# A GAT layer and a relational attention layer in one kernel: the second feed-forward's second product computed from seven products of quarters

## The chip, the cores and the metric

The kernel runs on one core of one Trainium2 chip. Five engines work side by side, each through its own list of instructions: TensorE (PE in the profile, its weight loads PEld), VectorE (DVE), ScalarE (ACT), GpSimd (POOL) and SyncE (SP), which here issues transfers. The metric is the time of one execution on the device in microseconds (us).

## The reference

64 graphs of 256 nodes with 256 features pass through two layers. In what follows, `x` is [64, 256, 256] and `adj` a 0/1 matrix per graph, all in float32:

```python
# layer 0
h = gat(x, adj, W1, a1);  h = gat(h, adj, W2, a2)     # softmax of leaky_relu scores
h = layernorm(x + h)
h = layernorm(h + relu(h @ w_ff1 + b_ff1) @ w_ff2 + b_ff2)
# layer 1, 8 heads of 32, relations r = 0..3
attn = softmax(q k^T / sqrt(32))
out  = sum over r of (attn * (adj == r)) @ v_r
x  = layernorm(h + out @ Wo + bo)
ff = gelu(x @ W1 + b1) @ W2 + b2        # 256 -> 1024 -> 256: W2 is what the change is about
return layernorm(x + ff)
```

## The kernel before, in words

Two graphs make a unit: 512 rows, in T = 4 blocks of 128 tokens, and there are NG = 32 units. `turn(y_, x_, z)` (L1021 to L1128) runs 32 times and works on three units at once: y does the attention and the second feed-forward (layer 1), x = y+1 the first feed-forward, z = y+2 the two GAT steps. `y`, `X["y"]` and so on are also the names of the residual rows of such a unit, [128, 4, 256], to which each stage adds in place. A prologue ahead of the turns (the fill) does units 0 and 1 and folds the scales and shifts of the layer norms into the weights, in pieces (`folding`, advanced by `next(fold)`).

A turn starts with `queries_keys` (qp, kp), then the scores of one graph and four heads at a time (sp, exponentials e, masked ea, sums es), the values (vp, v), the sums over the heads (po, zo), and, between these, x's first product (h1p). Then come z's projection (xpp), y's output product (yop), x's second product (yfp with wf), y's first product of the second feed-forward, then z's second GAT step, and y's second product (yfp with w).

The first product of the second feed-forward (`hidden_seven`, L789 to L870) already takes Strassen's seven products of quarters: the weights' combinations are made once in the fill (`seven`), those of the moving features by VectorE in each turn, and the results are added by VectorE and ScalarE from two PSUM banks per half. The second product (`hidden_out_block`, L872 to L882) is the plain one: for each block of 128 tokens eight matmuls over the 1024 hidden features, each with 128 tokens as the stationary operand and 256 columns of w2 moving; a float32 matmul shows as two records in the trace. At the end of each pair of blocks VectorE adds the bank to y (L882).

In the last part of a turn, the order is as follows. `hidden_seven` ends with z's `gat_first` between its parts. x's rows are normed (`normed`, L752 to L771: statistics and their aggregate by VectorE, rs by GpSimd, nm by VectorE, four scalings y by ScalarE), and brought into feature order by `normed_features` (four VectorE transposes into yt, then 16 moves of 32-row blocks, as SP transfers where `natural` is set). x's `affine` (rg2, rb2; two VectorE operations of 128x1024) follows, then z's `second_scores` (rows by TensorE, softmax by ScalarE and VectorE, which ends by scaling hp). `finish` norms and writes out the unit y-1, which was put in `waiting` a turn before. Then the product of y goes through its four blocks, and ahead of the last block `second_sums(z)` runs: ygp, two adds to z's rows, z's first norm, and `normed_features`, in which 4 of the 16 moves are GpSimd copies hT<-yt and 12 are SP transfers. These transposed rows of z are wanted in the middle of the next turn. z's next affine (rg1, rb1) comes after y's second norm there.

The order on PE and SP is the order of the program's text. On VectorE, ScalarE and GpSimd a scheduler chooses it from the times that it expects; `with behind(mark)` holds an instruction back until the marked one has been issued. PSUM has six banks that are shared in turn (tag "g"), and two more (po, zo). A matmul that takes a bank waits until the reader of what was in it has finished. Tiles of a tag with two buffers (`work`) are reused in turn in the same way.

The last two units differ: unit 30's product is cut into `pieces`, which are drawn one at a time within the last turn, and unit 31 has none beside it.

Of the kernel before, what the change touches and what calls it, by code (L numbers as in the profile page):

```python
# [9 lines left out]
F32 = mybir.dt.float32  # L10
# [375 lines left out]
def narrow_path(  # L386
# [97 lines left out]
    def columns(vs, name, queue):  # L484

        ns = [v.shape[0] // P for v in vs]
        rows = work.tile([P, KB * N], F32, tag="rz", name=f"{name}r")[:, 0:P]
        t = const.tile([P, sum(ns)], F32, name=name)
        at, views = 0, []
        for v, n in zip(vs, ns):  # L490
            queue.dma_start(rows[at:at + n, :], v.rearrange("(c p) -> c p", p=P))
            views.append(t[:, at:at + n])
            at += n
        ps = bank(f"{name}p")
        nc.tensor.transpose(ps[:, :at], rows[:at, :], ident[:at, :at])
        nc.vector.tensor_copy(t, ps[:, :at])
        return views
# [61 lines left out]
    def seven(w, name):  # L559
# [8 lines left out]
        nc.gpsimd.tensor_tensor(a21, a11, a21, ALU.subtract)  # L568
        return a11, a12, a22, s1, s2, a21, s4


    def shifted(w, blocks, shift, bias, name):
        ps = bank(f"{name}sp{blocks[0]}")
# [8 lines left out]
        for k in range(KB):  # L582
            nc.gpsimd.tensor_scalar(w[:, k], w[:, k], scale[:, k:k + 1], 1.0, op0=ALU.mult, op1=ALU.mult)

    w1s = []

    def folding():

        shifted(wf1, range(FB // 2), lb1, bf1, "bf1")
        yield  # L590
        shifted(wf1, range(FB // 2, FB), lb1, bf1, "bf1")
        scaled(wf1, lg1)
        yield
# [12 lines left out]
        shifted(w1, range(FB // 2, FB), lb3, b1, "b1")  # L606
        scaled(w1, lg3)
        w1s.extend(seven(w1, "w1"))
        yield

    fold = folding()


    for rb, v, name in ((rb1, g_bf2, "rbf2"), (rb2, t_bo, "rbo"), (rb3, t_b2, "rbt2")):
        nc.gpsimd.tensor_add(rb, rb, row(v, name, work.tile([P, KB * N], F32, tag="rz", name=name)[:, :F]))


    mark = {}
# [8 lines left out]
    def to_features(src, name):  # L627

        dst = work.tile([P, KB, TN], F32, tag="hT", name=name)
        for k in range(KB):  # L630
            ps = bank(f"{name}p{k}")
            for t in range(T):
                nc.tensor.transpose(ps[:, t * P:(t + 1) * P], src[:, t, k * P:(k + 1) * P], ident)
            nc.vector.tensor_copy(dst[:, k, :], ps)
        return [dst[:, k] for k in range(KB)]

    def adjacency(u, aq):
# [5 lines left out]
    def normed_features(u, l, xn, natural=False, queues=(nc.sync,)):  # L643
# [7 lines left out]
        if natural:  # L651
            hT = work.tile([P, KB, TN], F32, tag="hT", name=f"hT{u}_{l}")
            to = hT.rearrange("c k (t a r) -> c (k t) a r", a=Q, r=32)
            for q in range(Q):
                for a in range(Q):
                    nc.sync.dma_start(to[q * 32:(q + 1) * 32, :, a],
                                      yt[a * 32:(a + 1) * 32, q].rearrange("c k t r -> c (k t) r"))
            return [hT[:, k] for k in range(KB)]
        hT = work.tile([P, Q, KB, T, 32], F32, tag="hT", name=f"hT{u}_{l}")
        n = 0  # L660
# [80 lines left out]
    def add_blocks(u, name, y, b, lhs, rhs, n):  # L741

        ps = bank(f"{name}{u}_{b}")
        for i in range(NB):
            t = b * NB + i
            for k in range(n):
                nc.tensor.matmul(ps[:, i * F:(i + 1) * F], lhs(t, k), rhs(b, k),  # L747
                                 start=(k == 0), stop=(k == n - 1))
        yb = y[:, b * NB:(b + 1) * NB, :].rearrange("p t f -> p (t f)")
        nc.vector.tensor_tensor(yb, ps, yb, ALU.add)  # L750

    def normed(u, l, y, blocks=range(T)):  # L752

# [36 lines left out]
    def hidden_seven(u, l, hT, w, bi, func, h1):  # L790
# [58 lines left out]
        for h in halves:  # L849
            product(two[h], h, s1, moving(0), True)  # L850
            p5[h] = copied(h, 1, two[h])
        for h in halves:
            product(two[h], h, s4, quarter[1][1], False)
            copied(h, 0, two[h])
# [8 lines left out]
        for h in halves:  # L863
            product(one[h], h, s3, moving(2), False)
            added(h, 1, 1, p5[h])
        yield
        for h in halves:
            product(one[h], h, a22, moving(3), False)
            done(h, 1, 0, one[h])
            done(h, 1, 1)  # L870

    def hidden_out_block(u, l, y, h1, wo_, t):  # L872
        b, i = divmod(t, NB)
# [6 lines left out]
        if i == NB - 1:  # L880
            yb = y[:, b * NB:(b + 1) * NB, :].rearrange("p t f -> p (t f)")
            nc.vector.tensor_tensor(yb, ps, yb, ALU.add)  # L882

    hidden_ps = {}

# [65 lines left out]
                             start=True, stop=True)  # L951

    def divided(u, b, po, zo, oT):
        rz = work.tile([P, KB * N], F32, tag="rz", name=f"rz{u}_{b}")
        nc.vector.reciprocal(rz, zo)  # L955
        nc.vector.tensor_tensor(oT[:, :, b * N:(b + 1) * N],
                                po.rearrange("p (m n) -> p m n", m=KB),
# [25 lines left out]
    def first_scores(z):  # L983
        first_rows(z)
        first_softmax(z)

    def second_scores(z):
        d = g[z]
        d["s"] = gat_softmax(z, 1, d["hp"], score_rows(z, 1, d["hp"], F), F + 1, F, d["aT"])

    def second_sums(x_, on_tensor=False):
        d = g[x_]
# [9 lines left out]

    left = []

    def out_pieces(u, y, h1):

        for t in range(T):
            hidden_out_block(u, 1, y, h1, w2, t)
            b, i = divmod(t, NB)
            if i == NB - 1:  # L1010
                finish(u, y, b, 1)
            yield

    def finish(u, y, b, n):

        bt = slice(b * NB, (b + n) * NB)
        normed(u, 3, y, range(b * NB, (b + n) * NB))
        with behind("added"):
            affine(y[:, bt, :], rg4, rb4)
        nc.sync.dma_start(out[G * u + b:G * u + b + n].rearrange("b (c p) f -> p (b c) f", p=P), y[:, bt, :])  # L1020

    def piece():
# [3 lines left out]
    def turn(y_, x_, z):  # L1026
# [19 lines left out]
        def first_hidden(blocks):  # L1046
            if X:
                X["h1"] = hidden(x_, 0, X["hT"], wf1, bf1, AF.Relu, blocks, X.get("h1"))

        scores(0)  # L1050
        v = values(y_, hT, range(T))
# [46 lines left out]
            if Z and n > 1:  # L1098
                Z["hp"] = gat_first(z, Z["s"], Z["xp"], Z.get("hp"), range(2 * n - 4, 2 * n - 2))
        if X:  # L1100
            with behind("copied"):
                normed(x_, 1, X["y"])
            X["hT"] = (normed_features(x_, 1, X["y"], natural=True) if Z
                       else to_features(X["y"], f"h2T{x_}"))
            with behind("added"):
                affine(X["y"], rg2, rb2)
        if Z:
            checked(z, Z["aq"])
        if z + 1 < NG:
            load_adjacency(z + 1)  # L1110
        if Z:
            second_scores(z)
        if waiting:
            with behind("scaled" if Z else "copied"):
                finish(*waiting.pop(), 0, G)
        if y_ >= NG - 2:
            last = out_pieces(y_, y, h1)
            if X:
                left.append(last)
            else:  # L1120
                for _ in last:
                    pass
            return
        for t in range(T):
            if t == T - 1:
                second_sums(z)
            hidden_out_block(y_, 1, y, h1, w2, t)
        waiting.append((y_, y))  # L1128

    waiting = []  # L1130
# [4 lines left out]
    with tc.manual_schedule(engines={mybir.EngineType.PE, mybir.EngineType.SP}):  # L1135
# [18 lines left out]
        h1 = hidden(0, 0, g[0]["hT"], wf1, bf1, AF.Relu, range(FB))  # L1154
        hidden_out(0, 0, g[0]["y"], h1, wf2)
        normed(0, 1, g[0]["y"])
        next(fold)
        second_sums(1)
        g[0]["hT"] = to_features(g[0]["y"], "h2T0")
        affine(g[0]["y"], rg2, rb2)  # L1160
        for u in range(NG):
            turn(u, u + 1, u + 2)

# [53 lines left out]
```

## Time and profile before

| | us |
|---|---|
| median of 3 runs | 3192.44 (3191.73 to 3194.73) |
| profiled execution, time | 3190.37 |
| profiled execution, span | 3188.7 |
| mean granted TensorE clock in it | 0.993 of full speed |
| one turn (382.26 to 478.84, from the start of y's second product to that of the next) | 96.6 |
| VectorE busy | 2117.7 (66% of the span) |
| ScalarE busy | 1547.8 (49%) |
| GpSimd busy | 412.1 (13%) |

In the profile's rows, "yfp<-w,h" is y's second product, "yfp<-wf,h" that of x, L878 the line of both; "x2048" counts records, and "128*128 128x256" gives the tile of the stationary operand and the shape of the result. "idle before <-releaser" is what the engine waited for just ahead of the instruction. A row of the timeline has start, length, engine, line, operation, names and count; matmuls are pipelined, so the length of a row of them runs over the start of the next row a little, and the time that a row takes is best read from start to start. The waits of the whole kernel that belong to the places of the change:

```profile
POOL rs L763 <- DVE mv L762: 1743.8, 97, 52.1
ACT y L768 <- DVE nm L765: 420.2, 69, 20.8
POOL hT L665 <- DVE yt L648: 166.1, 56, 3.6
DVE nm L765 <- POOL rs L764: 160.6, 129, 2.1
ACT k L899 <- PE kp L897: 47.2, 62, 1.0
PEld h1a L820 <- DVE h L830: 16.6, 33, 1.2
PE qp L897 <- DVE h2T L634: 6.3, 2, 6.0
```

Its columns are: who waits, for whom, the sum in us, how many times, the longest. None of the first five is a wait of TensorE.

### The profile page before, as it was taken

To read this page: it belongs to the slowest core of one execution; us is meant where nothing else is said; L and a number is where in the kernel's file an instruction comes from. 1 tells how busy PE (TensorE), PEld (TensorE's weight loads), DVE (VectorE), ACT (ScalarE), POOL (GpSimd) and SP (SyncE) were. 2 spreads that over 40 slices of the span, in tenths; PEclk is the share of its full clock that TensorE was granted. 3 is DMA by queue.
4 is the path that set the end of the run, shared out by engine and by line. 5 is a ranking of instruction groups with operands and counts; after the bars stand their busy time and mean duration, and the time that the engine had idled before them with its cause. 6 is when DMAs were issued, how large, how long until landed. Compare 5 with 4: busy or idle time off the path is not lost.

```text
span 3188.7 us, 46935 instructions
## 1 busy us (share of the span) xinstructions
PE 3137.3 (98%) x17584; PEld 2178.4 (68%) x17584; DVE 2117.7 (66%) x3870; ACT 1547.8 (49%) x3076; POOL 412.1 (13%) x633
## 2 busy tenths in 40 slices
PE   8899999999999999999999999999999999999997
PEld 5577766677766677666677666777666776667755
DVE  3566666666676666676666666666766666766655
ACT  4255544555544545545545445554445455455543
POOL 1111011011011111110110110110101111101100
PEclk9999999999999999999999999999999999999999
DMA  5011112121111121121211121211112111211000
GB/s 144 19 37 37 21 35 44 39 44 29 26 39 40 42 44 26 24 43 39 44 37 22 34 44 39 44 29 24 40 39 44 40 28 25 44 39 31 24 12 15
DMA packets 461160, 117.09 MB, mean 37 GB/s; under 512 B 397400, under 2 KB 460288, under 8 KB 460928
## 3 DMA queue, kind: packets, MB, share of 16 engines
q1 hardware_dynamic: 450592, 106.60, 15.4%
q10 hardware_dynamic: 9280, 6.39, 0.7%
q8 instruction: 141, 2.31, 0.3%
q0 software_dynamic: 1056, 1.05, 0.1%
q14 instruction: 91, 0.75, 0.1%
HBM read 57.04 MB, written 16.78 MB: 23 GB/s over the span
## 4 chain that ended last, share of the span: by engine, by line
PE 91%; DVE 4%; ACT 1%; POOL 1%; DMA 1%; ACTq 1%; issue 1%; SPq 0%; DVEq 0%; POOLq 0%
PE yfp L878 24%; PE h1p L785 14%; PE po L947 7%; PE vp L910 7%; PE h1a L820 6%; PE sp L926 4%; PE h1b L820 4%; PE qp L897 4%; PE yop L747 4%; PE kp L897 3%; PE hpp L736 3%; PE xpp L694 3%; PE ygp L747 3%; PE zo L950 2%; POOL rs L764 1%; DVE st L761 1%
## 5 line engine op out<-in xcount | busy, mean ns | idle before, releaser
L934 DVE TENSOR_TENSOR ea<-e,aT 128x1024 f32<-128x1024 f32 x256 | 302.2, 1222 | 285.1 <-ACT e L932 285.1
L768 ACT ACTIVATE y<-y,nm,rs 128x256 f32<-128x256 f32 x512 | 269.4, 591 | 420.2 <-DVE nm L765 420.2
L878 PE MATMUL yfp<-w,h 128*128 128x256 f32 x2048 | 452.9, 379 | 0.0
L785 PE MATMUL h1p<-hT,wf 128*128 128x512 f32 x992 | 450.6, 602 | 0.0
L878 PE MATMUL yfp<-wf,h 128*128 128x256 f32 x2048 | 448.5, 380 | 0.0
L878 PEld LDWEIGHTS yfp<-wf,h 128*128 128x128 f32 x2048 | 387.8, 191 | 52.2 <-issue 0.5
L878 PEld LDWEIGHTS yfp<-w,h 128*128 128x128 f32 x2048 | 386.6, 190 | 51.9 <-DVE v L912 0.3
L932 ACT ACTIVATE e<-sp 128x512 f32<-128x512 f32 x512 | 263.7, 603 | 224.4 <-PE sp L926 218.1
L785 PEld LDWEIGHTS h1p<-hT,wf 128*128 128x128 f32 x992 | 180.6, 189 | 228.7 <-issue 193.1
L648 DVE STREAM_TRANSPOSE yt<-y 128x256 f32<-128x256 f32 x368 | 151.7, 431 | 214.7 <-ACT y L768 201.0
L787 ACT ACTIVATE h<-h1p,cols 128x512 f32<-128x512 f32 x256 | 172.8, 692 | 239.0 <-PE h1p L785 239.0
L763 POOL TENSOR_SCALAR rs<-mv 128x4 f32<-128x4 f32 (+1 forms) x130 | 29.1, 232 | 1751.0 <-DVE mv L762 1743.8
L955 DVE RECIPROCAL rz<-zo 128x512 f32<-128x512 f32 x64 | 214.7, 3354 | 53.6 <-PE zo L950 53.6
L665 POOL COPY hT<-yt 32x256 f32<-32x256 f32 x248 | 215.8, 870 | 191.9 <-DVE yt L648 166.1
L775 DVE TENSOR_TENSOR y<-y,rg 128x1024 f32<-128x1024 f32 (+1 forms) x130 | 157.0, 1209 | 98.5 <-ACT y L768 94.2
L910 PE MATMUL vp<-wv,hT 128*128 128x512 f32 x480 | 214.0, 599 | 0.0
L761 DVE BATCH_NORM_STATS2 st<-y 128x6 f32<-128x256 f32 x512 | 195.3, 408 | 4.5
L826 ACT COPY cp<-h1b 128x512 f32<-128x512 f32 x192 | 111.1, 581 | 113.4 <-PE h1b L820 70.1
L910 PEld LDWEIGHTS vp<-wv,hT 128*128 128x128 f32 x480 | 88.7, 190 | 110.4 <-issue 103.2
L776 DVE TENSOR_TENSOR y<-y,rb 128x1024 f32<-128x1024 f32 (+1 forms) x130 | 161.2, 1242 | 3.2
L830 DVE TENSOR_TENSOR h<-h1a,cp 128x512 f32<-128x512 f32 x192 | 130.3, 682 | 45.7 <-PE h1a L820 45.6
L696 ACT COPY xp<-xpp 128x260 f32<-128x260 f32 x128 | 47.6, 373 | 232.6 <-PE xpp L694 232.5
(183 smaller groups left out, 4773.1 us busy)
## 6 DMA issues: line engine op xcount, KB each, us to landing
hT<-yt SPq DMA_DIRECT2D x1038, 32.0 KB, 1.9
y<-in_x_dram SPq DMA_DIRECT2D x32, 512.0 KB, 4.0
xq<-in_x_dram SPq DMA_DIRECT2D x240, 64.0 KB, 2.3
aq<-in_adj_dram SPq DMA_DIRECT2D x240, 64.0 KB, 2.4
out_dram<-y SPq DMA_DIRECT2D x30, 512.0 KB
hT<-yt ACTq DMA_DIRECT2D x186, 32.0 KB, 1.9
wf<-in_L_gnn_w_ff_dram SPq DMA_DIRECT2D x2, 1024.0 KB, 7.1
w<-in_L_gnn_W_dram SPq DMA_DIRECT2D x2, 1024.0 KB
```

The costliest lines, as they stand in the source:

```text
L665: nc.gpsimd.tensor_copy(to, at)
L747: nc.tensor.matmul(ps[:, i * F:(i + 1) * F], lhs(t, k), rhs(b, k), start=(k == 0), stop=(k == n - 1))
L761: nc.vector.bn_stats(st[:, t, :], y[:, t, :])
L768: mark["normed"] = nc.scalar.activation(y[:, t, :], y[:, t, :], AF.Identity, bias=nm[:, t:t + 1], scale=rs[:, t:t + 1])
L785: nc.tensor.matmul(ps, wi[:, k, f * P:(f + 1) * P], hT[k], start=(k == 0), stop=(k == KB - 1))
L820: nc.tensor.matmul(ps[:, i * N:(i + 1) * N], w_[:, f * P:(f + 1) * P], m, start=first and i == 0, stop=True, skip_group_check=True)
L878: nc.tensor.matmul(ps[:, i * F:(i + 1) * F], h1[:, k, t * P:(t + 1) * P], wo_[:, k, :], start=(k == 0), stop=(k == FB - 1))
L897: nc.tensor.matmul(ps, w[:, k, m * P:(m + 1) * P], hT[k], start=(k == 0), stop=(k == KB - 1))
L910: nc.tensor.matmul(ps, hT[k][:, t * P:(t + 1) * P], wvf[:, k, :], start=(k == 0), stop=(k == KB - 1))
L932: nc.scalar.activation(e[:, a, :], ps[a], AF.Exp, scale=isd)
L934: nc.vector.tensor_tensor(ea[:, a:a + 2, :], e[:, a:a + 2, :], ab[:, None, :].to_broadcast([P, 2, NB * N]), ALU.mult)
L947: nc.tensor.matmul(po[hp, m * N:(m + 1) * N], vs[:, hp], w[:, a, j * N:(j + 1) * N], start=(n == 0), stop=(n == len(terms) - 1))
```

## The change

The second product of the second feed-forward is computed from seven products of quarters, too (`hidden_out_seven`). The hidden features h1 are cut into four quarters (first or second half of the 1024 features, first or second graph of the unit); VectorE makes four combinations s1, s2, s4, s3 of them in each turn, of 128x1024 elements, and the weights' combinations t1, t2, t3, t4 are made once by GpSimd in the fill (`seven_out`). A product is eight matmuls with 128 tokens stationary and 128 columns of weights moving, into one bank. Products 1, 4, 6 and 7 share one bank, 3 and 5 another, product 2 has its own; a product that adds to a bank starts after VectorE has added what was there before to the residual rows.

Around it:
- z's ygp sums come after the sixth product, where they came ahead of the last quarter of the plain one, and z's `second_softmax` is issued after the third.
- x's norm is behind the mark "fifth" in place of "copied"; of the 16 moves of its features the four with equal source and target rows become GpSimd copies.
- x's affine (rg2, rb2), and after it the `finish` of unit y-1, are issued after the products, behind the marks "summed" (the last add of ygp) and "quarters" (s3).
- done(h, 1, 1) in `hidden_seven` stands one part earlier.
- `to_features`, which takes transposes by TensorE out of PSUM in the fill and at the end, copies by ScalarE in place of VectorE; in the fill, `next(fold)` of the last part comes behind it; in turn 31 the pieces of unit 30 are drawn in more places.
- the tag "rz" has one buffer in place of two.

```diff
@@ -568,6 +568,18 @@
         nc.gpsimd.tensor_tensor(a21, a11, a21, ALU.subtract)
         return a11, a12, a22, s1, s2, a21, s4
 
+    def seven_out(w, name):
+
+        h = F // 2
+        b11, b12, b21, b22 = (w[:, k * FB // 2:(k + 1) * FB // 2, o * h:(o + 1) * h]
+                              for k in range(2) for o in range(2))
+        t1, t2, t4 = (const.tile([P, FB // 2, h], F32, name=f"{name}t{n}") for n in (1, 2, 4))
+        nc.gpsimd.tensor_tensor(t1, b12, b11, ALU.subtract)
+        nc.gpsimd.tensor_tensor(t2, b22, t1, ALU.subtract)
+        nc.gpsimd.tensor_tensor(t4, b21, t2, ALU.subtract)
+        nc.gpsimd.tensor_tensor(b12, b22, b12, ALU.subtract)
+        return b11, b21, b22, t1, t2, b12, t4
+
 
     def shifted(w, blocks, shift, bias, name):
         ps = bank(f"{name}sp{blocks[0]}")
@@ -582,7 +594,7 @@
         for k in range(KB):
             nc.gpsimd.tensor_scalar(w[:, k], w[:, k], scale[:, k:k + 1], 1.0, op0=ALU.mult, op1=ALU.mult)
 
-    w1s = []
+    w1s, w2s = [], []
 
     def folding():
 
@@ -606,13 +618,14 @@
         shifted(w1, range(FB // 2, FB), lb3, b1, "b1")
         scaled(w1, lg3)
         w1s.extend(seven(w1, "w1"))
+        w2s.extend(seven_out(w2, "w2"))
         yield
 
     fold = folding()
 
 
     for rb, v, name in ((rb1, g_bf2, "rbf2"), (rb2, t_bo, "rbo"), (rb3, t_b2, "rbt2")):
-        nc.gpsimd.tensor_add(rb, rb, row(v, name, work.tile([P, KB * N], F32, tag="rz", name=name)[:, :F]))
+        nc.gpsimd.tensor_add(rb, rb, row(v, name, work.tile([P, KB * N], F32, tag="rz", name=name, bufs=1)[:, :F]))
 
 
     mark = {}
@@ -631,7 +644,7 @@
             ps = bank(f"{name}p{k}")
             for t in range(T):
                 nc.tensor.transpose(ps[:, t * P:(t + 1) * P], src[:, t, k * P:(k + 1) * P], ident)
-            nc.vector.tensor_copy(dst[:, k, :], ps)
+            nc.scalar.copy(dst[:, k, :], ps)
         return [dst[:, k] for k in range(KB)]
 
     def adjacency(u, aq):
@@ -653,8 +666,8 @@
             to = hT.rearrange("c k (t a r) -> c (k t) a r", a=Q, r=32)
             for q in range(Q):
                 for a in range(Q):
-                    nc.sync.dma_start(to[q * 32:(q + 1) * 32, :, a],
-                                      yt[a * 32:(a + 1) * 32, q].rearrange("c k t r -> c (k t) r"))
+                    move = nc.gpsimd.tensor_copy if q == a else nc.sync.dma_start
+                    move(to[q * 32:(q + 1) * 32, :, a], yt[a * 32:(a + 1) * 32, q].rearrange("c k t r -> c (k t) r"))
             return [hT[:, k] for k in range(KB)]
         hT = work.tile([P, Q, KB, T, 32], F32, tag="hT", name=f"hT{u}_{l}")
         n = 0
@@ -747,7 +760,7 @@
                 nc.tensor.matmul(ps[:, i * F:(i + 1) * F], lhs(t, k), rhs(b, k),
                                  start=(k == 0), stop=(k == n - 1))
         yb = y[:, b * NB:(b + 1) * NB, :].rearrange("p t f -> p (t f)")
-        nc.vector.tensor_tensor(yb, ps, yb, ALU.add)
+        mark["summed"] = nc.vector.tensor_tensor(yb, ps, yb, ALU.add)
 
     def normed(u, l, y, blocks=range(T)):
 
@@ -849,6 +862,7 @@
         for h in halves:
             product(two[h], h, s1, moving(0), True)
             p5[h] = copied(h, 1, two[h])
+        mark["fifth"] = mark["copied"]
         for h in halves:
             product(two[h], h, s4, quarter[1][1], False)
             copied(h, 0, two[h])
@@ -863,11 +877,11 @@
         for h in halves:
             product(one[h], h, s3, moving(2), False)
             added(h, 1, 1, p5[h])
+            done(h, 1, 1)
         yield
         for h in halves:
             product(one[h], h, a22, moving(3), False)
             done(h, 1, 0, one[h])
-            done(h, 1, 1)
 
     def hidden_out_block(u, l, y, h1, wo_, t):
         b, i = divmod(t, NB)
@@ -880,6 +894,54 @@
         if i == NB - 1:
             yb = y[:, b * NB:(b + 1) * NB, :].rearrange("p t f -> p (t f)")
             nc.vector.tensor_tensor(yb, ps, yb, ALU.add)
+
+    def hidden_out_seven(u, l, y, h1, w, s1, s2, s3, s4):
+
+
+        b11, b21, b22, t1, t2, t3, t4 = w
+        K2, F2 = FB // 2, F // 2
+        a11, a12, a21, a22 = (h1[:, k * K2:(k + 1) * K2, b * N:(b + 1) * N]
+                              for b in range(2) for k in range(2))
+        nc.vector.tensor_tensor(s1, a21, a22, ALU.add)
+        nc.vector.tensor_tensor(s2, s1, a11, ALU.subtract)
+        nc.vector.tensor_tensor(s4, a12, s2, ALU.subtract)
+        mark["quarters"] = nc.vector.tensor_tensor(s3, a11, a21, ALU.subtract)
+
+        def product(ps, a, w_, first):
+            for i in range(NB):
+                for k in range(K2):
+                    nc.tensor.matmul(ps[:, i * F2:(i + 1) * F2], a[:, k, i * P:(i + 1) * P], w_[:, k, :],
+                                     start=first and i == 0 and k == 0, stop=True, skip_group_check=True)
+
+        def added(b, o, ps):
+            yq = y[:, b * NB:(b + 1) * NB, o * F2:(o + 1) * F2]
+            nc.vector.tensor_tensor(yq, ps[:, :F].rearrange("p (i f) -> p i f", i=NB), yq, ALU.add)
+
+        n = f"{l}_{u}"
+        one = bank(f"yf1{n}")
+        product(one, a11, b11, True)
+        added(0, 0, one)
+        yield
+        two = bank(f"yf3{n}")
+        product(two, s1, t1, True)
+        added(1, 1, two)
+        yield
+        ps = bank(f"yf2{n}")
+        product(ps, a12, b21, True)
+        added(0, 0, ps)
+        yield
+        product(one, s2, t2, False)
+        added(0, 1, one)
+        yield
+        product(two, s4, b22, False)
+        added(0, 1, two)
+        yield
+        product(one, s3, t3, False)
+        added(1, 1, one)
+        yield
+        product(one, a22, t4, False)
+        added(1, 0, one)
+        yield
 
     hidden_ps = {}
 
@@ -984,9 +1046,16 @@
         first_rows(z)
         first_softmax(z)
 
+    def second_rows(z):
+        g[z]["rows"] = score_rows(z, 1, g[z]["hp"], F)
+
+    def second_softmax(z):
+        d = g[z]
+        d["s"] = gat_softmax(z, 1, d["hp"], d["rows"], F + 1, F, d["aT"])
+
     def second_scores(z):
-        d = g[z]
-        d["s"] = gat_softmax(z, 1, d["hp"], score_rows(z, 1, d["hp"], F), F + 1, F, d["aT"])
+        second_rows(z)
+        second_softmax(z)
 
     def second_sums(x_, on_tensor=False):
         d = g[x_]
@@ -1002,21 +1071,25 @@
 
     left = []
 
-    def out_pieces(u, y, h1):
-
-        for t in range(T):
-            hidden_out_block(u, 1, y, h1, w2, t)
-            b, i = divmod(t, NB)
-            if i == NB - 1:
-                finish(u, y, b, 1)
+    def out_pieces(u, y, h1, last):
+
+
+        if u == NG - 2:
+            s = [work.tile([P, T, N], F32, tag="s", name=f"sq{u}_{n}") for n in range(2)]
+            s += [io.tile([P, T, N], F32, tag=t, name=f"sq{u}_{t}", bufs=1) for t in ("xq", "aq")]
+        else:
+            s = [work.tile([P, HPB, NB * N], F32, tag=t, name=f"{t}q{u}")[:, :, i * N:(i + 1) * N]
+                 for t in ("e", "ea") for i in range(2)]
+        for n, _ in enumerate(hidden_out_seven(u, 1, y, h1, w2s, *s)):
+            if last and n in (4, 6):
+                finish(u, y, n // 6, 1)
             yield
 
     def finish(u, y, b, n):
 
         bt = slice(b * NB, (b + n) * NB)
         normed(u, 3, y, range(b * NB, (b + n) * NB))
-        with behind("added"):
-            affine(y[:, bt, :], rg4, rb4)
+        affine(y[:, bt, :], rg4, rb4)
         nc.sync.dma_start(out[G * u + b:G * u + b + n].rearrange("b (c p) f -> p (b c) f", p=P), y[:, bt, :])
 
     def piece():
@@ -1046,6 +1119,8 @@
         def first_hidden(blocks):
             if X:
                 X["h1"] = hidden(x_, 0, X["hT"], wf1, bf1, AF.Relu, blocks, X.get("h1"))
+            else:
+                piece()
 
         scores(0)
         v = values(y_, hT, range(T))
@@ -1098,33 +1173,34 @@
             if Z and n > 1:
                 Z["hp"] = gat_first(z, Z["s"], Z["xp"], Z.get("hp"), range(2 * n - 4, 2 * n - 2))
         if X:
-            with behind("copied"):
+            with behind("fifth"):
                 normed(x_, 1, X["y"])
             X["hT"] = (normed_features(x_, 1, X["y"], natural=True) if Z
                        else to_features(X["y"], f"h2T{x_}"))
-            with behind("added"):
-                affine(X["y"], rg2, rb2)
         if Z:
             checked(z, Z["aq"])
         if z + 1 < NG:
             load_adjacency(z + 1)
         if Z:
-            second_scores(z)
-        if waiting:
-            with behind("scaled" if Z else "copied"):
-                finish(*waiting.pop(), 0, G)
-        if y_ >= NG - 2:
-            last = out_pieces(y_, y, h1)
-            if X:
-                left.append(last)
-            else:
-                for _ in last:
-                    pass
+            second_rows(z)
+        pieces = out_pieces(y_, y, h1, y_ >= NG - 2)
+        if y_ == NG - 2:
+            left.append(pieces)
+            affine(X["y"], rg2, rb2)
+            finish(*waiting.pop(), 0, G)
             return
-        for t in range(T):
-            if t == T - 1:
+        for n, _ in enumerate(pieces):
+            if Z and n == 2:
+                second_softmax(z)
+            if Z and n == 5:
                 second_sums(z)
-            hidden_out_block(y_, 1, y, h1, w2, t)
+        if not X:
+            return
+        with behind("summed", "quarters"):
+            affine(X["y"], rg2, rb2)
+            if waiting:
+                with behind("scaled"):
+                    finish(*waiting.pop(), 0, G)
         waiting.append((y_, y))
 
     waiting = []
@@ -1154,10 +1230,10 @@
         h1 = hidden(0, 0, g[0]["hT"], wf1, bf1, AF.Relu, range(FB))
         hidden_out(0, 0, g[0]["y"], h1, wf2)
         normed(0, 1, g[0]["y"])
-        next(fold)
         second_sums(1)
         g[0]["hT"] = to_features(g[0]["y"], "h2T0")
         affine(g[0]["y"], rg2, rb2)
+        next(fold)
         for u in range(NG):
             turn(u, u + 1, u + 2)
```

More of the change, by code (lines that the diff above doesn't have):

```diff
@@ L486, in columns @@
         ns = [v.shape[0] // P for v in vs]
-        rows = work.tile([P, KB * N], F32, tag="rz", name=f"{name}r")[:, 0:P]
+        rows = work.tile([P, KB * N], F32, tag="rz", name=f"{name}r", bufs=1)[:, 0:P]
         t = const.tile([P, sum(ns)], F32, name=name)
@@ L953, in divided @@
     def divided(u, b, po, zo, oT):
-        rz = work.tile([P, KB * N], F32, tag="rz", name=f"rz{u}_{b}")
+        rz = work.tile([P, KB * N], F32, tag="rz", name=f"rz{u}_{b}", bufs=1)
         nc.vector.reciprocal(rz, zo)
```

## The prediction, before the result was known

> **What bounds the kernel.** I read the page's shares and chain of waits, then its groups, then one steady turn in the timeline, engine by engine, and at last the fill.
>
> ```profile
> PE 3137.3 (98%) x17584; PEld 2178.4 (68%) x17584; DVE 2117.7 (66%) x3870; ACT 1547.8 (49%) x3076; POOL 412.1 (13%) x633
> ```
> ```profile
> PE 91%; DVE 4%; ACT 1%; POOL 1%; DMA 1%; ACTq 1%; issue 1%; SPq 0%; DVEq 0%; POOLq 0%
> ```
>
> TensorE bounds it: 98% busy, 91% of the chain. Whatever shortens its stream pays at once; whatever makes it wait costs in full. The last rows of the turn that begins at 382.26 us:
>
> ```profile
> 478.68 10.53 PE L878 MATMUL yfp<-w,h 128*128 128x256 f32 x48
> 489.04 3.62 PE L747 MATMUL ygp<-hp,s 128*128 128x256 f32 x16
> 492.50 3.62 PE L878 MATMUL yfp<-w,h 128*128 128x256 f32 x16
> ```
>
> Here 48 records of the product take 10.36 us (to the start of the next row), the ygp sums lie inside, and the last 16 records take 3.45. So the product costs 13.81 us per unit, 64 records of 0.216. The next turn starts at 495.95. The last quarter is also a cover: between ygp's end and qp the other engines have 3.45 us to norm the unit z. A boundary in full (592.54 is a qp start), TensorE first:
>
> ```profile
> 592.54 3.60 PE L897 MATMUL qp<-hT,wq 128*128 128x512 f32 x8
> 595.97 3.60 PE L897 MATMUL kp<-hT,wk 128*128 128x512 f32 x8
> 599.50 1.15 PE L926 MATMUL sp<-q,k 32*128 32x256 f32 x16
> 600.57 7.13 PE L910 MATMUL vp<-wv,hT 128*128 128x512 f32 x16
> 607.64 0.50 PE L926 MATMUL sp<-q,k 32*128 32x256 f32 x4
> ```
> ```profile
> 592.67 0.23 POOL L763 TENSOR_SCALAR rs<-mv 128x4 f32<-128x4 f32 x1 [9.12 <-DVE mv L762]
> 592.99 1.03 POOL L764 TENSOR_TENSOR rs<-rs,mhalf 128x4 f32<-128x4 f32 x1
> 597.03 3.60 POOL L665 COPY hT<-yt 32x256 f32<-32x256 f32 x4 [3.01 <-DVE yt L648]
> ```
> ```profile
> 594.25 2.07 ACT L768 ACTIVATE y<-y,nm,rs 128x256 f32<-128x256 f32 x4 [7.27 <-DVE nm L765]
> 596.23 1.24 ACT L899 ACTIVATE q<-qp,cols 128x512 f32<-128x512 f32 x2
> ...
> 599.60 0.69 ACT L899 ACTIVATE k<-kp,cols 128x512 f32<-128x512 f32 x1 [1.03 <-PE kp L897]
> ```
> ```profile
> 596.94 1.23 DVE L775 TENSOR_TENSOR y<-y,rg 128x1024 f32<-128x1024 f32 x1
> ```
>
> TensorE runs from qp to sp without a gap, though the first norm of z (rs, pow, nm, four y, four hT copies) lies across ScalarE, GpSimd and VectorE at that time: GpSimd is taken from 597.03 to 600.63, 4.5 to 8.1 us after qp's start. The fill:
>
> ```profile
> 107.58 5.83 PE L897 MATMUL qp<-h2T,wq 128*128 128x512 f32 x8 [5.99 <-DVE h2T L634]
> ```
>
> [...]the fill's load-only row shows one each 0.111 us ((1.86 - 0.19) / 15):
>
> ```profile
> 24.60 1.86 PEld L576 LDWEIGHTS bf1sp<-cols,wf 128*128 128x128 f32 x16
> ```
>
> [...]the trace's granted clock was 0.50 in 107.58 to 111.50, after 5.99 us idle.
>
> **The change, part by part.**
>
> *The product.* Seven products of 8 matmuls of 128 moving columns[...]: 112 records for 64. Full overlap gives 0.111 each (128-column transposes, rows L703, come every 0.11), 12.4 us: a gain of 1.4 per unit. Bounds: [...]no overlap at all (0.111 + 0.109) 24.6. I take 0.111, since rows with 256 columns already show 0.216, exactly two such loads, hence no gap beside the stream. A stall of 0.2 us per turn at h1a (its load waits for a VectorE add; 16.6 us in 33 products) goes as the order of marks changes: gain 1.65 per turn.
>
> *VectorE.* Four combinations of 128x1024 at 1.22, seven adds of 128x256 at some 0.42, less two adds of 0.66: +6.5 us per unit, its share 66% to about 70%. In the tail I followed each: s1 is ready at about the rows' end and p2 needs it 1.8 later; s2, s4, s3 end by 482.1; p6's bank is freed some 0.8 before it is needed. Hidden. The sums' scaled hp comes at 488 to 488.8, ygp wants it at 489.3. Hidden.
>
> *Transposed features.* Four of 16 SP DMAs of x's normed features become GpSimd copies (870 ns each). They land some 14 us before qp wants them, against 2 before. No time, either way.
>
> *What leaves the tail.* This decides. x's second affine (2 x 1.23, VectorE) and the whole finish of unit y-1 (statistics, rs, high, pow, nm, four y, two affines, the output's DMA) are issued behind the last pieces: in the next turn's start. And only the seventh product (8 matmuls, 1.78 us) covers between ygp and qp. The built order is the same at all 29 boundaries:
> - GpSimd: rs, pow of z; four hT copies; then rs, high, pow of the finish.
> - ScalarE: q0; four y of z; q1; k0; four y of the finish; k1; four e.
> - VectorE: rg2, z's statistics, rb2, nm, the finish's statistics between four yt, rg1, nm of the finish, rb1, rg4, rb4, ea, es, v.
>
> With qp's start as 0: ygp's second add -1.57; rg2 until 0.2; z's statistics until 1.5; rs and pow until 3.1; nm 3.25; four y until 5.4; yt until 6.5; copies until 10.2 (GpSimd); rs, high, pow of the finish until 11.6; nm, then four y until 13.9; k1 until 14.5. vp1 takes kp1's bank, so TensorE waits from 9.8 to 14.6. Behind it VectorE has rb1 until 13.0, rg4 and rb4 (from the second y, 13.9) until 16.4, ea 18.7, es 19.8, v0 20.4, v1 21.1. The fourth sp of scores(1) wants v1's bank: it ends at 22.05 where unhindered it would at 16.17. Delay 5.9 us per boundary. Bounds: if copies start as early as in the trace (4.5) and VectorE is no limit, k1 ends at about 12.4: 2.7. Above: the idle of 4.8 us can halve the clock[...]; the v1 wait absorbs most, 0.3 more.
>
> *Fill and end.* ScalarE takes the transposes from PSUM, and the w1 folding moves behind: qp of turn 0 at about 101.3 instead of 107.58: -6 (-3 to -8). Last unit: p2 waits for s1, and the adds queue behind the norm: +1.5 net (-3 to +5).
>
> *Sum.* 29 x (5.9 - 1.65) = +123; turn 0 and unit 30 -3; fill -6; end +1.5: +116. On the profiled run (span 3188.7, time 3190.4): 3306. The median of the runs shown, 3192.4, lies 2 above it: 3308 to 3310; I say 3309.
>
> **Rivals.**
>
> A, the queues at the boundary as worked out: 3309; own range 3275 to 3345 (5.9 less or more 1.2 is 35 either way). Chance 0.72.
>
> B, the other side: the finish's norm isn't late, because GpSimd gets to its rs before the copies, or k1 gets to ScalarE in time. Then 30 x 1.65 + 6 - 1 stays: 3192 - 54 = 3138. It decides below (1.65 + 7.5/29) = 1.9 us per boundary. For it: the boundary of before runs without a gap with the same norm of z in it, and VectorE has a third of its time free. Against: [...]the finish stands ahead of k1 in ScalarE's. 0.09.
>
> C, no full overlap for 128 columns: at 0.135 per record the product takes 15.1, 2.7 a turn above A: 3309 + 86 = 3395. For it: twice the loads per column streamed, PEld's share rises. Against: 0.216 for 256 columns. 0.09.
>
> D, the stall is there but near its lower bound, 2.7 to 3.5: 3192 + 29 x (1.05 to 1.85) - 7 = 3215 to 3240. For it: what VectorE does in the stall would otherwise come later, and slack further on may take some. 0.10.
>
> **How the numbers follow.** The likeliest, A, gives 3309. C and the lower part of B stay out; the range for 8 in 10 takes A and the upper half of D, 3230 to 3350. Within 0.2% (6.4 us, what a measurement of this kernel can tell from no change) counts as same. Faster is B without its upper edge, 0.09; same is the edge between B and D, 0.02; slower is the rest, 0.89.
>
> **What would show it.** Right: rows of vp with idle before them put down to ScalarE's k, and of sp put down to VectorE's v, together 4 to 7 us per turn; the finish's rs on GpSimd just behind four hT copies; the seven products within 12.2 to 12.8 us; TensorE's share down to some 93%. Wrong: if qp, vp and sp still run gap-free (then B), if a record of the new product takes over 0.12 (C), or if p2 to p7 wait for VectorE in the tail, which I have at none.

## The result: 3363.6 us, 5.4% slower, and the profile after

| | before | after |
|---|---|---|
| median | 3192.09 us (4 runs) | 3363.61 us (4 runs, 3361.96 to 3367.82) |
| ratio to before | | 1.0537 (95% interval 1.0519 to 1.0556) |
| span of the profiled execution | 3188.7 us | 3360.3 us |
| mean granted clock of TensorE in it | 0.993 | 0.965 |
| start of turn 0 (its first qp) | 107.58 us | 110.98 us |
| a steady turn | 96.58 us | 102.40 us |

The way was the one forecast, the size was not: the forecast was 3309 with 3350 as its upper end. The page of the changed kernel, its shares and its chain by engine:

```profile
PE 3187.6 (95%) x19120; PEld 2226.1 (66%) x19120; DVE 2307.4 (69%) x4146; ACT 1543.9 (46%) x3088; POOL 465.3 (14%) x757
...
PE 82%; DVE 7%; POOL 5%; ACT 4%; issue 2%; DMA 1%; SPq 0%; DVEq 0%; ACTq 0%; POOLq 0%
```

TensorE's share of the chain fell from 91% to 82%; VectorE, GpSimd and ScalarE, 6% of it before, have 16%. Its timeline at one boundary of turns (start, length, then what it is; in brackets the idle time and who ended it; eq and eaq hold the combinations of h1, w2t those of the weights):

```profile
389.61 1.95 PE L913 MATMUL yf<-w,h 128*128 128x128 f32 x16
391.40 1.95 PE L913 MATMUL yf<-w2t,eq 128*128 128x128 f32 x16
393.19 1.95 PE L913 MATMUL yf<-w,h 128*128 128x128 f32 x16
394.97 1.95 PE L913 MATMUL yf<-w2t,eq 128*128 128x128 f32 x16
396.76 3.74 PE L913 MATMUL yf<-w,eaq 128*128 128x128 f32 x32
400.33 3.62 PE L760 MATMUL ygp<-hp,s 128*128 128x256 f32 x16
403.79 1.95 PE L913 MATMUL yf<-w2t,h 128*128 128x128 f32 x16
405.57 3.60 PE L959 MATMUL qp<-hT,wq 128*128 128x512 f32 x8
409.01 3.60 PE L959 MATMUL kp<-hT,wk 128*128 128x512 f32 x8
412.77 1.15 PE L988 MATMUL sp<-q,k 32*128 32x256 f32 x16 [0.17 <-ACT k L961]
413.85 1.98 PE L972 MATMUL vp<-wv,hT 128*128 128x512 f32 x4
419.65 8.33 PE L972 MATMUL vp<-wv,hT 128*128 128x512 f32 x12 [3.82 <-ACT k L961]
427.91 1.15 PE L988 MATMUL sp<-q,k 32*128 32x256 f32 x16
```

The seven products follow each other without a gap, 16 records in 1.79 us, 0.112 each. Then vp stops for ScalarE's k (k1, the second one), and the 12 records after that take 8.26 us to the next row, where 12 of them took three quarters of 7.07 us before. The same kernel in stretches of time around this wait (for each engine busy us and instructions, then the granted clock, DMA's share, GB/s):

```profile
412.77:415.60 2.83, 2.83 (x20) 1.40 (x20) 0.94 (x1) 0.00 (x0) 2.62 (x6) 1.00 0.13 35
415.60:419.65 4.05, 0.23 (x1) 0.00 (x0) 1.89 (x3) 2.70 (x6) 1.12 (x2) 0.89 0.20 54
419.65:423.06 3.41, 3.41 (x4) 1.51 (x5) 3.38 (x4) 1.88 (x4) 0.00 (x0) 0.50 0.22 72
423.06:427.91 4.85, 4.85 (x9) 1.77 (x7) 3.78 (x5) 0.00 (x0) 0.00 (x0) 0.74 0.57 180
```

The clock was halved in the first stretch after the wait and for part of the next (asked for 418.70 to 425.55, the trace gives 0.50, and 1.00 before and after): that is the other part of the loss. What the wait waited for, on GpSimd and on ScalarE:

```profile
407.12 1.04 POOL L776 TENSOR_SCALAR rs<-mv 128x4 f32<-128x4 f32 x1 [9.26 <-DVE mv L775]
408.24 1.03 POOL L777 TENSOR_TENSOR rs<-rs,mhalf 128x4 f32<-128x4 f32 x1
412.57 2.69 POOL L678 COPY hT<-yt 32x256 f32<-32x256 f32 x4 [3.30 <-DVE mv L775]
415.36 0.23 POOL L776 TENSOR_SCALAR rs<-mv 128x4 f32<-128x4 f32 x1
415.56 0.19 POOL L784 TENSOR_TENSOR high<-high,mv 128x4 f32<-128x4 f32 x1
415.70 1.02 POOL L777 TENSOR_TENSOR rs<-rs,mhalf 128x4 f32<-128x4 f32 x1
```
```profile
416.95 2.07 ACT L781 ACTIVATE y<-y,nm,rs 128x256 f32<-128x256 f32 x4 [4.23 <-DVE nm L778]
418.93 0.67 ACT L961 ACTIVATE k<-kp,cols 128x512 f32<-128x512 f32 x1
```

The finish's rs stands behind z's four copies, its four y stand ahead of k1, and TensorE's second vp wants k1's bank: it starts 14.08 us after qp. The difference of the two profiled spans, 171.6 us, by place, from the starts of qp in both traces: start of turn 0 +3.4; turns 0 and 1 (no wait yet) -2.8; turns 2 to 29 +156.3 (5.58 each); turn 30 +7.6; the last turn +7.1. The start of turn 0 is made of two opposite parts. In the fill one set of vectors is transposed late:

```profile
23.22 0.28 PE L495 MATMUL colsp<-ident,colsr 32*128 32x32 f32 x1 [8.75 <-DMA wo<-in_L_gnn_Wo_dram]
```

In the kernel before:

```profile
14.26 0.31 PE L495 MATMUL colsp<-ident,colsr 32*128 32x32 f32 x1
```

From the fill's first hidden product (h1p) to qp, on the other hand, 39.5 us go by in place of 46.3.

### The profile page after: what moved, and what is told of

It reads as the page before. It is cut to its first block, busy times and chain, and to the rows that moved or that the text cites. A ratio compares the mean times of both kernels' runs of the same rounds, so it can differ in the third digit from the quotient of the medians.

```text
span 3360.3 us, 50547 instructions
## 1 busy us (share of the span) xinstructions
PE 3187.6 (95%) x19120; PEld 2226.1 (66%) x19120; DVE 2307.4 (69%) x4146; ACT 1543.9 (46%) x3088; POOL 465.3 (14%) x757
## 4 chain that ended last, share of the span: by engine, by line
PE 82%; DVE 7%; POOL 5%; ACT 4%; issue 2%; DMA 1%; SPq 0%; DVEq 0%; ACTq 0%; POOLq 0%
PE h1p L798 14%; PE yfp L892 13%; PE yf L913 10%; PE vp L972 8%; PE po L1009 7%; PE h1a L833 6%; PE h1b L833 5%; PE yop L760 3%; PE hpp L749 3%; PE xpp L707 3%; PE sp L988 3%; PE ygp L760 3%; ACT y L781 2%; POOL rs L777 2%; DVE st L774 2%
## 5 line engine op out<-in xcount | busy, mean ns | idle before, releaser
L972 PE MATMUL vp<-wv,hT 128*128 128x512 f32 x480 | 308.0, 801 | 111.2 <-ACT k L961 111.2
L776 POOL TENSOR_SCALAR rs<-mv 128x4 f32<-128x4 f32 (+1 forms) x130 | 54.5, 419 | 1947.6 <-DVE mv L775 1930.9
L972 PEld LDWEIGHTS vp<-wv,hT 128*128 128x128 f32 x480 | 117.7, 258 | 286.6 <-issue 151.1
L678 POOL COPY hT<-yt 32x256 f32<-32x256 f32 x248 | 188.3, 759 | 196.8 <-DVE mv L775 96.1
L778 DVE SCALAR_TENSOR_TENSOR nm<-mv,rs 128x4 f32<-128x4 f32 (+1 forms) x130 | 21.1, 163 | 211.8 <-POOL rs L777 211.8
L988 PEld LDWEIGHTS sp<-q,k 32*128 32x128 f32 x2048 | 92.7, 184 | 109.5 <-issue 72.8
L961 ACT ACTIVATE q<-qp,cols 128x512 f32<-128x512 f32 x64 | 43.3, 677 | 254.6 <-PE qp L959 254.6
L999 DVE TENSOR_TENSOR es<-e 128x1024 f32<-128x1024 f32 x128 | 156.0, 1219 | 0.0
```

What stands on the lines that cost most here:

```text
L972: nc.tensor.matmul(ps, hT[k][:, t * P:(t + 1) * P], wvf[:, k, :], start=(k == 0), stop=(k == KB - 1))
```

## The experiments

Twelve kernels ran, each beside the kernel before on the same chip. Except where said, the diff is against the changed kernel.

**Taking the copies out of GpSimd's queue** (copies_sp).

```diff
-                if q == a:
+                if q == a and l != 0:
                     nc.gpsimd.tensor_copy(to, at)
```

> The changed kernel, but the four hT<-yt copies of a unit's first norm (0.67 us each on GpSimd at the boundary) are SP transfers, so that the finish's rs and pow no longer stand behind them. Queue theory (A): rs of the finish runs at about 6.9 us after qp's start instead of 9.8, its y on ScalarE end at about 10.5 instead of 13.45, k1 ends at 11.1, vp1 starts at 11.2 instead of 14.1: a gap of 1 to 1.5 instead of 4[...]. VectorE's queue (rg4, rb4, ea, es, v) then sets the second sp at some 18 to 19 instead of 22.3. A turn is 98 to 99 us instead of 102.4, the whole 3240 to 3270. Rival (the product of quarters itself, or VectorE's added work, is what costs): 3364, unchanged.

3268.1 us (ratio 1.0231, 1.0214 to 1.0248), a turn 98.8 or 99.3. The 99.3 come with a lower clock after the wait (last section): in the turn shown below the granted clock was 0.70 from 414.00 to 419.60, and 1.00 before and after. The wait at vp fell to 2.2 us beyond the usual spacing of its records, 2.0 of them put down to k:

```profile
415.18 7.11 PE L972 MATMUL vp<-wv,hT 128*128 128x512 f32 x12 [2.04 <-ACT k L961]
```

That is nearly 1 more than expected, since the finish's rs, now held only by VectorE's statistics, took 1.13 us where 0.23 was reckoned:

```profile
409.98 1.13 POOL L776 TENSOR_SCALAR rs<-mv 128x4 f32<-128x4 f32 x1 [3.40 <-DVE mv L775]
411.08 0.19 POOL L784 TENSOR_TENSOR high<-high,mv 128x4 f32<-128x4 f32 x1
411.23 1.02 POOL L777 TENSOR_TENSOR rs<-rs,mhalf 128x4 f32<-128x4 f32 x1
```

Four copies out of GpSimd's queue are worth 95 us, with what they do to the clock: so much of the loss is the queue's, with the seven products in place. The 2 us that still are waited for, and the rest of the 3268, this run leaves open.

**Keeping TensorE busy while it waits** (busy). Nothing is removed; 18 useless records (BUSY is 9, and a matmul is two records) are added per turn:

```diff
         for t in blocks:
+            if t == 1:
+                d = psum.tile([P, 512], F32, tag="zo", name=f"busy{u}")
+                for _ in range(BUSY):
+                    nc.tensor.matmul(d[:, :F], ident, wv[:, 0, 0, :], start=True, stop=True)
             ps = bank(f"vp{u}_{t}")
```

> The changed kernel with 9 matmuls of 128x256 (18 records, 3.9 us) of no use put between the first and second vp of each turn, so that TensorE is not idle while it waits for k1. Nothing else is moved. Theory that half of the loss beyond the forecast is the halved clock after the wait: vp1 still starts at 14.1 after qp, but the 12 records of vp run in 5.2 us instead of 8.3, and the second sp starts when v1 is there, at about 20.8 instead of 22.3: 1.3 to 2 us per turn less, 3364 - 29 x 1.6 = about 3317. Rival (the clock is no term, the queues alone set the start of sp): no change, 3364, or slower where the first turns without a wait pay 3.9 us.

3323.6 us (1.0405, 1.0388 to 1.0423): 40 us faster by added work. TensorE's timeline of this run:

```profile
424.37 4.05 PE L973 MATMUL busy<-wv,ident 128*128 128x256 f32 x18
428.36 5.42 PE L976 MATMUL vp<-wv,hT 128*128 128x512 f32 x12
433.70 2.33 PE L993 MATMUL sp<-q,k 32*128 32x256 f32 x16
```

The second vp starts 14.08 us after qp (414.28) as before, but the 12 records take 5.34, and the mean granted clock of the run is 0.993 for 0.965. Then sp takes 2.26 for 1.08: here it waits for v, as the forecast had it. A turn is 100.57, so the halved clock costs 1.83 a turn of 102.40. (vp's 12 records lost 2.9 us by it; some 1.1 of that would have been waited for v anyway.) What is left over the 95.30 of an unhindered turn, the changed kernel's turn 1, is 5.27: the queues' own delay.

**The rows of the fill** (fill_rows).

```diff
-        rows = work.tile([P, KB * N], F32, tag="rz", name=f"{name}r", bufs=1)[:, 0:P]
+        rows = work.tile([P, HPB, NB * N], F32, tag="ea", name=f"{name}r")[:, 0, 0:P]
...
-        nc.gpsimd.tensor_add(rb, rb, row(v, name, work.tile([P, KB * N], F32, tag="rz", name=name, bufs=1)[:, :F]))
+        nc.gpsimd.tensor_add(rb, rb, row(v, name, work.tile([P, HPB, NB * N], F32, tag="ea", name=name)[:, 0, :F]))
```

> The changed kernel with the vectors' rows of the fill in tiles of tag ea (two buffers) in place of rz (one buffer). Theory: the single rz buffer holds the transfer of the second set of rows back until the first has been transposed (colsp starts at 23.2 us instead of 14.3), and all the fill behind it is late by that: 9 to 10 us less, 3354. Rival (the transfer of wo or w2 was late for another reason, such as the order of the queues): within 2 us of 3364.

3355.3 us (1.0505, 1.0487 to 1.0522). In its timeline the transpose is back in its place:

```profile
14.46 0.31 PE L495 MATMUL colsp<-ident,colsr 32*128 32x32 f32 x1
```

Turn 0 starts 7.6 us earlier, at 103.35. The single buffer of rz, an edit that had been left out of the sum, made the transpose late by 8.8 us and h1p by 7.7 of its 10.3. The other 2.6 mean nothing: up to turn 0 the kernel before and before_late (below) have the same instructions in the same order on every engine, and h1p starts at 61.26 us in the one trace and at 66.76 in the other. So a few us in the fill can't be told from a single trace. The effect of rz stands beside that: h1p starts at 63.8 to 65.7 in the four kernels with the rows in ea, and at 68.7 or later in the eight that have the change's single buffer.

**The two other edits in the fill** (features_dve, fold_early).

```diff
-            nc.scalar.copy(dst[:, k, :], ps)
+            nc.vector.tensor_copy(dst[:, k, :], ps)
```

> The changed kernel with to_features copying by VectorE again, as in the kernel before (the fill's and the last turns' transposes). If ScalarE's copies are what shortened the way from the fill's first hidden product to qp of turn 0 (39.4 us after the change, 46.3 before): that way is 43 to 46 us again and the whole 3 to 7 us longer, 3367 to 3371. Rival (the moved folding is what shortened it): within 2 us of 3364.

The second kernel has `next(fold)` back between x's norm and `second_sums(1)`.

> The changed kernel with the last part of the folding (b1sp on TensorE, the scaling and the combinations of the weights on GpSimd, an add on VectorE) ahead of the second unit's sums in the fill, as before. If the moved folding shortened the fill: qp of turn 0 is 2 to 7 us later, 3366 to 3371. Rival (ScalarE's copies did): within 2 us of 3364. Both may hold in part.

3370.9 us (1.055, 1.0532 to 1.0567) and 3366.7 us (1.0537, 1.052 to 1.0555); the second lies within the spread of the changed kernel's own runs, so the traces have to tell. The way from h1p to qp was 43.4 us with VectorE's copies and 44.6 with the early folding, for 39.5 (39.3 to 40.5 in the kernels that keep both edits): both were needed for the 6.9 us that the fill gained there. With VectorE's copies h1p itself starts 5.7 us later, which a single trace doesn't show to be theirs, and turn 30 is 2.3 us shorter.

**The finish out of the boundary, later** (finish_late).

```diff
+        if waiting:
+            with behind("exps"):
+                finish(*waiting.pop(), 0, G)
```

This stands in the next turn behind `first_hidden(range(2, 5))`, "exps" marks the last exponential of `weighted`, and both old calls of finish at the end of the turn are gone.

> The changed kernel with the finish of unit y-1 issued in the middle of the next turn, its instructions held behind the exponentials of the third scores. Queue theory: no wait at vp1, clock at full, a turn is about 95.2 us: 3364 - 29 x 7.1 = about 3158, faster than the kernel before. Rival (VectorE, with 6.5 us more work per unit, or the product of quarters takes the time wherever the finish lies): over 3250.

3169.9 us (0.9922, 0.9905 to 0.9938), 0.8% faster than the kernel before. TensorE's timeline:

```profile
408.74 1.15 PE L988 MATMUL sp<-q,k 32*128 32x256 f32 x16 [0.28 <-ACT k L961]
409.81 7.13 PE L972 MATMUL vp<-wv,hT 128*128 128x512 f32 x16
416.88 1.40 PE L988 MATMUL sp<-q,k 32*128 32x256 f32 x16
418.20 1.07 PE L1009 MATMUL po<-e,v 128*32 128x256 f32 x16
```

No wait at vp, a mean granted clock of 0.991, and a turn of 95.66. The rest over the expected 95.2 is at both sp.

**The finish in the last part of the turn, as in the kernel before** (finish_tail): after `second_softmax(z)`, so behind the third product, and behind the mark "scaled".

> The changed kernel with the finish of unit y-1 back in the last part of the same turn, behind the scaling of hp, where the kernel before had it; x's affine stays late. Queue theory: the boundary's queues hold no finish, vp1 does not wait, a turn is 95.3 to 95.8 us, the whole about 3165 to 3175. Rival (the last part of the turn is too full for it on VectorE with the four combinations and the seven adds, so that a bank or ygp waits there): TensorE waits at yf or ygp, 97 to 100 us a turn, 3200 to 3300.

3174.3 us (0.9932, 0.9915 to 0.9948), a turn 95.71. So the last part of the turn had room for the finish and the combinations of quarters together, and moving the finish out of it bought next to nothing.

**The moved finish with the plain product** (plain): in the changed kernel the four blocks of `hidden_out_block` in place of the seven products, z's softmax after the first block, ygp ahead of the last.

> The changed kernel with the plain second product (32 matmuls of 256 columns, 13.8 us, no combinations of quarters, two adds instead of seven) in the place of the seven products; the finish still lies at the turn's start, and the built order has it ahead of both k on ScalarE. If the place of the finish is the cause whatever the product: TensorE waits 4 to 6 us at sp or vp behind a k, the clock halves, a turn is 102 to 105 us, the whole 3340 to 3430. Rival (the stall needs the seven products: the shorter cover behind ygp, 1.8 us for 3.45, or VectorE's added work): a turn of 97 to 99 us, 3200 to 3270.

3420.4 us (1.0705, 1.0687 to 1.0723): worse than the change. With the plain second product the stall is there, too, at sp instead of vp, since this build has the finish's y ahead of both k:

```profile
412.32 3.60 PE L958 MATMUL kp<-hT,wk 128*128 128x512 f32 x8
421.31 2.09 PE L987 MATMUL sp<-q,k 32*128 32x256 f32 x16 [5.39 <-ACT k L960]
```

So the finish at the turn's start makes the stall, whatever the product, and finish_late and finish_tail, which move it alone, have none. The other work sent to that place, x's affine, no run takes away while the finish stays. In the changed kernel its two operations start on VectorE at 404.60, ahead of z's last statistics, and at 406.87, where z's rs runs beside it (last section), so it can have a part in the 5.3 us; with the finish gone it costs 0.6 us a turn (best_qk_affine). How much the shorter cover behind ygp adds can't be read from this pair, as the two builds order ScalarE differently.

**The kernel before with the late finish** (before_late, against the kernel before: the call of finish moved as in finish_late, and its `affine` no longer behind "added").

> The kernel before with the finish in the middle of the next turn, as in the run finish_late. If the gain of finish_late over the kernel before (0.9 us a turn) is the product of quarters: 3192, within 5. Rival (the tail of the kernel before is relieved by the move and the product adds nothing): about 3170.

3185.8 us (0.9972, 0.9961 to 0.9983), between the two: a turn of 96.37 for 96.58. The 0.2 us wait at h1a is gone (1.4 us in all, for 16.6), and it is back in finish_tail (15.1): it comes and goes with the finish in the last part, by what way was not traced. Its turn 30 is 1.7 us shorter, where a last turn 3.3 us longer takes it back. Its turn 0 starts 6.4 us later, with the same instructions ahead of it: this is the fill's own spread. Against it finish_late has 0.71 us a turn less: that is what the change gives net in a turn, once the finish is in the same place in both. The product of quarters saves 1.30 (12.51 us for 13.81) and loses 0.35 ahead of the first sp and 0.25 in the second.

**A version that beats both** (best, best_qk, best_qk_affine): finish_late with the rows of fill_rows and a piece of the last turn drawn later; then the query and key products in the order q0, k0, q1, k1; then x's affine held back like the finish:

```diff
+        if Y.pop("affine", None):
+            with behind("exps"):
+                affine(Y["y"], rg2, rb2)
...
-        with behind("summed", "quarters"):
-            affine(X["y"], rg2, rb2)
...
+        X["affine"] = True
```

> The run finish_late with the rows of the fill in tiles of tag ea, and with the third piece of unit 30's product drawn after the scores of the last turn instead of ahead of them, so that the scores' bank does not wait for an add that VectorE has behind a reciprocal (3.37 us, then half the clock). Fill theory: -7.4; the wait at the end: -3.4 to -5.5. Together 3157 to 3160. Rival (the gains hide one another): 3165 or more.

> The run best with the query and key products in the order q0, k0, q1, k1, so that the first scores' k0 does not wait on ScalarE behind q1. The first sp of a turn waits 0.28 us for k0 in best: 29 x 0.28 = 8 us less, 3153. Rival (what waits next takes it): 3159 or more.

> The run best_qk with x's affine (rg2, rb2) held behind the third scores' exponentials of the next turn as well. The second sp of a turn takes 1.40 us in best where it took 1.15 before, since v comes late on VectorE; with 2.4 us less ahead of it this goes: 29 x 0.25 = 7 us less than best_qk, 3146. Rival (VectorE pays it back in the middle of the turn): as best_qk or slower.

3161.2 us (0.9893, 0.9877 to 0.991), 3159.6 us (0.9888, 0.9872 to 0.9905) and 3143.0 us (0.9834, 0.9818 to 0.9851). The first is just over the expected 3157 to 3160: the 3.37 us wait of the last turn's scores was gone, but TensorE then waited 4.7 us at yop for VectorE, and the last turn was only 0.6 shorter. In best_qk the rival came true. The second sp of a turn in best_qk and in best_qk_affine:

```profile
407.98 1.75 PE L986 MATMUL sp<-q,k 32*128 32x256 f32 x16
```
```profile
407.77 1.15 PE L986 MATMUL sp<-q,k 32*128 32x256 f32 x16
```

The 0.3 us saved at k0 came back as a longer wait for v, since VectorE was the later of the two; with the affine out of its way both went, and a turn is 95.06.

## Why the prediction was wrong in size

**Right.** The product: 0.112 us per record for 0.111, and the load-only row of the fill has 0.111, too: beside the load the stream of 128 columns adds no time that the trace shows, and rival C is out. The wait at h1a went, though with the finish and not with the marks, and no product of a steady turn waits for the four combinations. That the engines would take the built order was the author's estimate; the trace has it on ScalarE, VectorE and GpSimd at all 29 boundaries. The queue was read almost in its times, too: k1 at 14.0 us for 14.5, vp at 14.1 for 14.6, and 5.3 us of delay from the queues (run busy) for 5.9. B, that the norm isn't late, fell; so did D: the wait alone is over its whole delay.

**Wrong: "the v1 wait absorbs most, 0.3 more".** This is the term of the sum that failed: the halved clock stood at nothing in the 5.9 and at 0.3 in its upper bound, and it costs 1.83 us a turn. The clock stayed at 0.50 for 6.8 us (418.70 to 425.55; what it lacks in the stretches above, 4.05 x 0.11 + 3.41 x 0.50 + 4.85 x 0.26 = 3.4, is 6.8 us at half), so that the 12 records of vp ended at 22.3 us, after v1 (20.6) and not before it. Over 29 turns that is 53 us; the queues' own delay, 5.27 for 5.9, gave 18 back. Taken together, a delay of 7.1 for 5.9 is 35 of the 55 us that are missing. The gain per turn came out at 1.3 net for 1.65 (the product saves 1.30 for 1.4, and the sp that waits 0.17 us for k0 was not in the sum): 10 more. Some 6 go the other way: the kernel before had a few turns of up to 97.9 us, which the changed one hasn't. So far the sum would be at about 3348, just inside the range; the fill and the last turn carried it out. The fill had a warning: the prediction has the clock at 0.50 after 5.99 us idle, but in that trace it was at 0.50 from 98.30 on, before that wait began, and in the course of one of 3.08 us.

**Wrong: "Fill and end", -6.** Its way from h1p to qp was -6.9, as forecast, by both edits; but the single buffer of rz held back the transfer of the vectors and gave +10.3 at h1p. That edit had been left out of the sum. Fill: +3.4 for -6 in these two traces, of which a few us are spread.

**Wrong: "Last unit ... +1.5".** The last turn was 7.1 longer. It has 3.4 us of wait at sp, where an add stands behind a reciprocal of 3.35 on VectorE, 1.74 at the second product and 1.47 at the last. What the cure of the first gained went for the most part into a longer wait at yop (best), so how much each costs by itself stays open.

## What to carry to other kernels

Work moved "out of the way" of a bottleneck lands in other engines' queues: write down, for each engine's queue at the new place, what stands behind it that the bottleneck wants, GpSimd's and ScalarE's too. A wait of TensorE can cost more than its length: here 4.0 us of it came with 6.8 us at a granted clock of 0.50, 1.83 us of each turn. So price the records behind it at half clock, too. Buffers taken from a set-up phase to make room are an edit with a price of their own.

## What the runs showed of the hardware

- The clock fell with waits much shorter than the 5.99 us of the fill. In copies_sp a wait of 2.2 us was followed by slow records in 10 of 29 turns (6.5 us for vp's last 11 intervals, 4.8 in the others); with 4.0 us in the changed kernel it was so in all 29 (7.6 to 7.8 us for 4.7 in the turns without the wait). The changed kernel's trace has 37 half-clock stretches, 32 of 6.83 us and 4 of 3.41, the last cut off by the end, and all its changes of the clock lie whole multiples of 3.413 us apart. Counted in such steps from a change of the clock in the trace of copies_sp, the 10 slow waits lie inside one step (the two latest end at its edge, within 0.02 us), and the other 19 lie across an edge. In the changed kernel all 29 lie across one and the clock fell, so what decides it is not shown by these two runs.
- The turns fall into step with the changes of the clock. In the changed kernel they run 102.20, 102.30, 102.35, 102.38 and settle at 102.40, 30 times 3.413; after a disturbed turn of 102.58 they begin again at 102.31. In plain they alternate between about 104.66 and 103.52, together 61 times 3.413.
- In the changed kernel GpSimd's rs took 1.04 us in place of 0.23 in all 30 cases in which it started beside an add of VectorE with rb (both operands in SBUF), ending 0.1 us after that; in no other of the 130. In copies_sp it was a multiplication with rg (409.79 to 411.02) that it ran beside, and it took 1.13. Beside adds with an operand in PSUM it took no more than 0.25 (h1a in 32 cases, ygp in one). In the changed kernel it put 0.8 us into the chain of the boundary which the forecast hadn't.
